# Cross-attention with residual and layer norm: the first chunk loaded in two transfers, the last eight pairs in a new order, the last store in two halves

## The chip, the cores and the metric

The kernel runs on one core of one Trainium2 chip. The metric is device time in microseconds (us) of one execution. Before the change it is 512.98 us, the median of three runs (512.11 to 513.15). Beside the runs there is one profiled execution, whose trace is what the pages below show. The engines are called PE (TensorE, matrix products; PEld is its weight load), DVE (VectorE), ACT (ScalarE), POOL (GpSimd) and SP (SyncE, which here only issues transfers).

## The reference

Queries come from `x` (4 × 2048 rows of 512), keys and values from a context of 4 × 77 rows of 512, with 16 heads of 32. All is float32.

```python
qs = (q @ wq).reshape(Bq, Lq, H, HD).transpose(0, 2, 1, 3)
ks_ = (k @ wk).reshape(Bq, Lk, H, HD).transpose(0, 2, 1, 3)
vs = (v @ wv).reshape(Bq, Lk, H, HD).transpose(0, 2, 1, 3)
scores = jnp.einsum('bhqd,bhkd->bhqk', qs, ks_) / jnp.sqrt(jnp.float32(HD))
scores = jnp.where(mask[:, None, :, :], -jnp.inf, scores)
attn_w = jax.nn.softmax(scores, axis=-1)
attn = jnp.einsum('bhqk,bhkd->bhqd', attn_w, vs)
attn = attn.transpose(0, 2, 1, 3).reshape(Bq, Lq, H * HD)
out = attn @ wo + q
mu = jnp.mean(out, axis=-1, keepdims=True)
var = jnp.mean((out - mu) ** 2, axis=-1, keepdims=True)
return (out - mu) / jnp.sqrt(var + EPS) * gamma + beta
```

## The kernel before, in words

**Tiling.** The 8192 rows of `x` are 64 tiles of 128 rows. Two tiles are a pair (32 pairs), four tiles a group (16 groups, one load of x transposed each). Each float32 factor of a big matrix product is split into a high and a low part, so each product is three matmuls (high·high, low·high, high·low) over four chunks of 128 of the inner 512.

**Order.** Nothing is scheduled by a program: the string `ORDER` is a list of words, one operation each, and every engine executes its own operations in the order of the words. The letter names the operation, the number the tile, pair or group. Further strings fix the buffer of each tile (`SLOTS`) and how many no-ops PE executes between the matmuls of a visit (`PADS`, one sign for each visit, in base 36).

**One tile.** A *visit* of 12 matmuls makes a block of queries for a group (`Q`, line 290; its copy out of PSUM is `q`, on DVE). `S` (line 414) makes a tile's scores in 64 small matmuls. `T` (DVE, line 431) adds the mask and takes the maxima of four heads, `e` (ACT, line 446) the exponentials of four heads with their sums, `r` (DVE, line 456) the reciprocals, `n` (POOL, line 461) the normalisation. `t` (DVE, line 482) transposes the probabilities in blocks of 32. `P` (line 493) regroups them by twelve transfers for each pair; the suffix s, a or g says from which queue, SP's, ACT's or POOL's. `V` (line 507) is the value product of a pair, in two PSUM banks; `a` (ACT, line 536) and `b` (DVE, line 540) split its result. `O` (line 579) is the output projection of a tile, a visit of 12 matmuls. `x` loads the rows of x; the residual is added by DVE on the way out (`+`, line 588), in PSUM by DVE (`$`, line 591), or by PE through an identity ahead of the projection (`X`, line 566).

**Layer norm.** Up to tile 47 it goes in pairs: `s` (DVE statistics), `v` (POOL), `k` (ACT scaling, line 617), `f` (POOL, gamma and beta, lines 621 and 622), `w` (store, SP, line 625). From tile 48 on it goes by single tiles: `s` at lines 630 and 632, `u` (POOL, lines 636 and 637), then either `%` (ACT, line 645) and `f`, or `y` (centring, DVE, line 649) and `z` (finish, DVE, line 652). `@` is `u` and the shift at line 641 together.

**The end.** The last pair's tiles are regrouped one by one: `U` (twelve transfers a tile, line 493 as well) and `W` (line 522), the value product of a single tile, with `c` and `d` in place of `a` and `b`. Tile 63 is normalised in two halves (`h`, `m`, lines 467 and 473).

**The start.** Seven matmuls on constants run first (lines 661 to 664), after three no-ops. SP issues the loads in this order: four chunks of "256 columns of x transposed and 512 of wq" (393 KB each, line 677), the context in two halves (315 KB each, line 679), four chunks of wk (262 KB each, line 681), the mask, the rest of the first x. ACT and DVE split chunk 0 (lines 694 to 699), PE makes the first queries chunk by chunk (line 702, twelve matmuls a chunk), then the keys (line 313).

## Time and profile before

| | us |
|---|---|
| median of three runs | 512.98 |
| the profiled execution's own time | 511.94 |
| its span in the trace | 510.10 |
| first matmul on data starts | 4.60 |
| last matmul ends | 503.43 |
| granted TensorE clock, mean | 0.998 |

The page of the profile gives the busy time of every engine over the span, and the chain of work that ended last. The answer of windows gives the same busy times for chosen stretches: length, then PE, PEld, DVE, ACT and POOL with their instruction counts, the granted clock, the mean busy share of the 16 DMA engines, and GB/s. A timeline row is start, duration, engine, line, operation, output and inputs, shapes, and a count when equal neighbours are drawn together; in brackets stands how long the engine had been idle and what released it. A row on SPq or ACTq is the issue of a transfer, not the transfer. Here the ACT operations around the last exponentials may serve as an example of reading:

```profile
477.72 0.34 ACT L446 ACTIVATE pbuf<-pbuf,nm 128x77 f32<-128x77 f32 x1
477.97 0.19 ACT L446 ACTIVATION_READ_ACCUMULATOR pbuf<-pbuf,nm 128x1 f32 x1
478.06 0.58 ACT L536 CAST AH<-pa 128x512 fp32r<-128x512 f32 x1
```

The last exponential of all is the one at 477.72; it ends with the reading of its sum at 478.16, and ACT goes on with a split of a value product.

### The profile page before, as it was taken

The numbers are of one execution on the slowest core, as the hardware profiler recorded it, in microseconds if no ns is written. First come the engines' busy times: TensorE is split into PE (matmuls) and PEld (weight loads), VectorE is DVE, ScalarE is ACT, GpSimd is POOL, SyncE is SP. The second block draws the span as 40 slices with busy tenths as digits, with TensorE's granted clock in tenths as the row PEclk, the third lists the DMA queues.
The fourth block names the chain that finished last, engine by engine and source line by source line (L and its number), as shares of the span: only waits on it lengthen the run. The fifth ranks groups of instructions, "written<-read, shape, count | busy, mean of one in ns | idle before, by whom it ended". The sixth has DMA issues, their size and how long they took to land.

```text
...
## 1 busy us (share of the span) xinstructions
PE 499.4 (98%) x6835; PEld 384.7 (75%) x6835; DVE 470.7 (92%) x2565; ACT 463.2 (91%) x2221; POOL 421.6 (83%) x389
## 2 busy tenths in 40 slices
...
GB/s 304 399 137 216 191 171 173 251 190 239 267 222 219 189 238 209 200 243 207 229 206 245 200 217 238 187 243 161 218 223 210 225 224 168 174 242 259 176 174 214
DMA packets 58995, 110.95 MB, mean 217 GB/s; under 512 B 9398, under 2 KB 11790, under 8 KB 58886
## 3 DMA queue, kind: packets, MB, share of 16 engines
...
## 4 chain that ended last, share of the span: by engine, by line
PE 79%; POOL 6%; DVE 5%; DMA 4%; ACT 2%; issue 1%; SPq 1%; DVEq 0%; POOLq 0%
PE pq L290 32%; PE po L579 25%; PE sc L414 10%; PE pa L507 9%; DMA PT<-B 3%; ACT pbuf L446 2%; DVE B L482 2%; PE pv L341 2%; POOL PT L493 1%; PE pk L313 1%; DMA stage_a<-wk 1%; DVE pbuf L431 1%; POOL o L621 1%; POOL mvt L637 1%; POOL o L622 1%
## 5 line engine op out<-in xcount | busy, mean ns | idle before, releaser
L446 ACT ACTIVATE pbuf<-pbuf,nm 128x77 f32<-128x77 f32 x1024 | 352.5, 351 | 4.2 <-DVE nm L431 4.0
L446 ACT ACTIVATION_READ_ACCUMULATOR pbuf<-pbuf,nm 128x1 f32 x1024 | 196.2, 192 | 0.0
L431 DVE CUSTOM_DVE_ANT_0 pbuf<-sc,mb 128x77 f32<-128x77 f32 x1024 | 171.3, 233 | 8.0 <-PE sc L414 4.3
L461 POOL TENSOR_TENSOR pbuf<-pbuf,ri 128x1232 f32<-128x1232 f32 x63 | 142.8, 2267 | 30.4 <-DVE ri L456 26.2
L579 PE MATMUL po<-woh,AH 128*128 128x512 f32 x256 | 102.2, 399 | 1.8 <-DVE nm L431 1.4
L290 PE MATMUL pq<-xth,wqh 128*128 128x512 f32 (+1 forms) x256 | 101.3, 396 | 0.3
L579 PE MATMUL po<-woh,AL 128*128 128x512 f32 x256 | 100.0, 391 | 0.2
L579 PE MATMUL po<-wol,AH 128*128 128x512 f32 x256 | 99.8, 390 | 0.0
L482 DVE STREAM_TRANSPOSE B<-pbuf 128x1280 f32<-128x1280 f32 x64 | 95.9, 1500 | 2.9 <-POOL pbuf L473 1.4
L290 PE MATMUL pq<-xtl,wqh 128*128 128x512 f32 (+1 forms) x256 | 98.1, 383 | 0.0
L290 PE MATMUL pq<-xth,wql 128*128 128x512 f32 (+1 forms) x256 | 98.1, 383 | 0.0
L431 DVE DVE_READ_ACCUMULATOR2_ANT nm<- 128x1 f32 x1024 | 84.7, 83 | 0.0
L273 POOL TENSOR_TENSOR xtl<-xtf,xth 128x1024 fp32r<-128x1024 f32 x28 | 67.2, 2406 | 5.8 <-ACT xth L269 5.8
L622 POOL TENSOR_TENSOR o<-o,bet 128x512 f32<-128x512 f32 x52 | 67.2, 1293 | 4.1
L414 PEld LDWEIGHTS sc<-kct,q 32*64 32x64 f32 x4096 | 51.3, 130 | 22.8 <-issue 10.8
L621 POOL TENSOR_TENSOR o<-o,gam 128x512 f32<-128x512 f32 x52 | 68.3, 1314 | 0.2 <-issue 0.2
L414 PE MATMUL sc<-kct,q 32*64 32x77 f32 x4096 | 60.7, 238 | 0.0
L507 PE MATMUL pa<-PT,vsb 96*32 96x256 f32 x992 | 59.7, 382 | 0.0
L579 PEld LDWEIGHTS po<-woh,AH 128*128 128x128 f32 x256 | 48.0, 188 | 14.8 <-PE pa L507 1.0
L290 PEld LDWEIGHTS pq<-xth,wqh 128*128 128x128 f32 x256 | 48.0, 188 | 12.4 <-issue 1.2
L579 PEld LDWEIGHTS po<-woh,AL 128*128 128x128 f32 x256 | 48.0, 188 | 11.5 <-DVE AL L540 1.4
L579 PEld LDWEIGHTS po<-wol,AH 128*128 128x128 f32 x256 | 48.1, 188 | 9.9 <-issue 0.5
...
## 6 DMA issues: line engine op xcount, KB each, us to landing
...
```

The source lines that it names most:

```text
L273: nc.gpsimd.tensor_tensor(l[:, c : c + 2], fx.pop((g, c)), xh[g][:, c : c + 2].bitcast(F32), ALU.subtract)
L290: nc.tensor.matmul(pq, w[:, c, m * P : (m + 1) * P], r[g][:, c, rs], start=(n == 0), stop=(n == 11))
L341: nc.tensor.matmul(pv[: rows.stop - rows.start], ctx_s[c][i][:, rows], v[c], start=(n == 0), stop=(n == 11))
L414: mm = nc.tensor.matmul(sc[j][r0 : r0 + SR, g * NK : (g + 1) * NK], qs[q, g, rs.start + r0 : rs.start + r0 + SR], kct[q, g, t // TPB, keys ...
L431: nc.vector.tensor_tensor_reduce(pb[:, h // 2, (h % 2) * NK : (h % 2 + 1) * NK], scs[t][j][:, g * NK : (g + 1) * NK], mb[:, t % TPB, keys_ ...
L446: nc.scalar.activation(pb[:, h // 2, (h % 2) * NK : (h % 2 + 1) * NK], pb[:, h // 2, (h % 2) * NK : (h % 2 + 1) * NK], AF.Exp, bias=nmax[t ...
L461: nc.gpsimd.tensor_tensor(pv, pv, rv.to_broadcast((P, NP, 2, NK)), ALU.mult)
L482: nc.vector.transpose(bt.rearrange("p c q r -> p q c r"), pbuf[t % NPB].rearrange("p q (c r) -> p q c r", c=5),)
L507: nc.tensor.matmul(pas[b, g // 2][HD * j : HD * (j + 1), (g % 2) * BLK : (g % 2 + 1) * BLK], vsb[:, 2 * b // TPB, h % 2, HD * (h // 2) : H ...
L579: nc.tensor.matmul(pos[t], a[:, c, rs], w[:, c, :], start=(first and c == 0 and n == 0), stop=(c == NC_D - 1 and n == 2),)
L621: nc.gpsimd.tensor_tensor(o, o, gam, ALU.mult)
L622: nc.gpsimd.tensor_tensor(o, o, bet, ALU.add)
```

## The change

It has three parts.

- **Start.** Chunk 0 is loaded by two transfers, 512 of its 768 columns by SP and the last 256 by ACT, ahead of ACT's table load. SP's order becomes context half 0, wk 0, wk 1, context half 1, wk 2, wk 3. Eight matmuls on constants follow one no-op, instead of seven after three.
- **Order.** `ORDER` is new from the transposes of tile 1 on to about pair 7, and from tile 52 to the end. Between these (tiles 18 to 50) the words are the same but for two loads and the slots. `PADS` and `SLOTS` are new accordingly: 1723 no-ops in all instead of 1468. In the last part tile 49's residual is added by DVE instead of PE, tile 48's scaling goes from ACT to DVE (`y48`, `z48`), and tile 62's transpose moves from ahead of tile 63's last exponentials to directly ahead of tile 63's transpose. The transfers are shared out anew: of the 24 of tiles 62 and 63, ACT's queue issues eleven (nine before).
- **End.** Tile 62's statistics come from two passes on ACT with accumulated sums (`=`, `stats_act`) instead of DVE's. Tile 63 is finished and stored in two halves of 256 columns (`>` and `<`), the first stored from SP's queue, the second from ACT's.

The diff, with `ORDER` cut to its changed beginning and end, and `SLOTS` left out:

```diff
-WARM = 7
+WARM = 8
...
 ORDER = """
 R1 R0 R3 E l0 l2 C2 C0 C1 C3 g5 M4.4 A0 M0.1 M12.4 A1 M1.3 A3 M8.4 K2 A2 H2 J3 p i3 g4 J1 K0 i2 S0 I2 j2 S1 T0.1
 e0.1 T0.2 H0 T0.0 j3 e0.0 T1.0 T0.3 e0.2 T1.1 Q4 T1.2 e0.3 F0 T1.3 I0 e1.2 r0 n0 S2 q4 e1.0 S3 T2.3 T2.0 Q7 i5 T2.1
-e1.3 F2 T2.2 j5 t0 e1.1 Q6 i4 F1 g7 r1 Y1 e2.0 F3 L1 T3.2 n1 Q5 x1 T3.1 e2.1 Y0 q6 R2 T3.3 e3.3 j4 t1 B0 e2.3 P0.6s
-x3 e3.1 B2 D0 i7 q7 Z0.s T3.0 P0.10s e3.0 q5 P0.2s S4 P0.7s D2 e3.2 Z3.s S6 T4.0 P0.4s e2.2 G1 B1 g6 G2 Z1.s G0
-Z2.s T4.3 e4.3 P0.3s r3 G3 P0.0s Q9 n3 T4.1 P0.1s T4.2 e4.2 P0.9s D1 P0.8s r2 n2 e4.0 t3 P0.5s Q8 P0.11s e4.1 T6.0
-T6.3 i6 t2 Q10 e6.0 r4 P1.0s T6.2 n4 P1.8s T6.1 e6.1 S5 P1.2s q10 x2 q8 Q11 e6.2 j6 P1.11s T5.3 P1.1s T5.2 e5.3
-P1.10s T5.1 P1.9s t4 j7 e6.3 P1.4s S7 P1.6s Q14 T7.0 P1.7s e7.0 q9 P1.3s r6 T7.3 P1.5s n6 e7.3 T7.2 x0 q11 Q13 g8
-e7.2 T5.0 Z13.s T7.1 g9 e7.1 Z6.s M16.4 Z10.s S9 q13 Z11.s e5.0 q14 V0 r7 t6 n7 e5.1 V1 a0.1 T9.1 e5.2 t7 Q15 a1.0
-b0.1 a1.1 P3.4s r5 T9.2 Z12.s n5 e9.2 b1.0 P3.1s b1.1 P3.8s O2 e9.1 T9.3 P3.2s t5 P3.0s a0.0 P3.5s i8 T9.0 P2.2s S8
-e9.0 +2 j8 P3.3s T8.3 O3 P2.6s e9.3 b0.0 P3.6s T8.1 P3.10s T8.2 i9 P2.8s r9 s2 P3.11s S10 e8.2 j9 P3.9s +3 O1 P3.7s
-T8.0 e8.0 P2.9s q15 s3 P2.3s n9 e8.1 P2.7s T10.0 P2.4s O0 T10.1 e8.3 x7 T10.2 v1 P2.1s +1 g11 e10.0 T10.3 P2.11s
...
+e1.3 F2 T2.2 j5 t0 e1.1 Q6 i4 F1 g7 r1 Y1 e2.0 F3 L1 T3.2 n1 Q5 x1 T3.1 e2.1 q6 T3.3 e3.3 j4 t1 B0 e3.2 T3.0 P0.4s
+q7 x2 e2.3 q5 P0.7s S4 D0 P0.5s e3.0 S6 P0.10s T4.3 P0.0s G0 B2 e3.1 R2 T4.0 g6 P0.2s e4.3 r3 P0.8s G3 n3 P0.11s B1
+e2.2 D2 P0.6s T4.1 T4.2 e4.1 G2 r2 Q8 i7 t3 x11 n2 P0.3s e4.2 P0.9s T6.0 P0.1s T6.2 e4.0 j7 x0 Q9 T6.3 Z13.s t2
+e6.0 Z0.s e6.3 G1 S5 r4 P1.0s T6.1 n4 e6.2 P1.7s q8 Q10 T5.3 P1.6s T5.0 P1.10s e6.1 T5.2 P1.3s T5.1 P1.5s i6 S7 t4
+P1.1s e5.3 Z1.s j6 Q11 P1.11s T7.2 e7.2 P1.9s T7.3 Z2.s q9 P1.8s e7.3 Q13 r6 D1 n6 P1.4s T7.0 P1.2s e7.0 T7.1 g9
+q10 x3 e7.1 Z12.s V0 q13 g8 q11 a0.0 Z11.s r7 e5.0 t6 V1 n7 Z10.s Z7.s e5.1 b0.0 S9 N t7 a1.1 Q12 e5.2 b1.1 P3.9s
+a1.0 P3.5s r5 T9.0 n5 P3.11s e9.0 b1.0 Q14 P3.3s T9.2 Z8.s e9.2 T9.1 P3.2s T9.3 P3.4s e9.3 t5 Y0 S8 P3.10s a0.1 O2
+P3.7s q12 i9 T8.1 P3.0s T8.0 e9.1 P2.3s T8.3 P3.8s q14 Z9.s e8.0 O3 T8.2 P3.1s b0.1 P3.6s e8.3 +2 Z5.s r9 P2.0s n9
+e8.2 S10 +3 P2.7s S11 P2.2s T10.0 e8.1 P2.9s s2 O1 j9 s3 T10.3 e10.3 r8 T10.1 v1 g10 Q15 +1 e10.1 Z4.s t9 P2.6s n8
...
-+45 n50 P24.4s s45 e51.2 g30 P24.0s S52 e51.1 +44 P24.5s P24.2g P24.11s V23 T52.0 i29 M56.4 T52.2 P24.10a j29 T52.3
-S53 a23.1 T52.1 e52.3 Q59 r51 t50 e52.1 n51 g31 P24.6s s44 a23.0 x60 Q58 T53.0 e52.2 P24.9s t51 P24.8s P24.1g e52.0
-P24.3s M60.4 P25.11s T53.2 Q57 P25.4s e53.0 q58 P25.5s r52 T53.1 n52 P25.1s e53.2 b23.0 P25.2s T53.3 S54 P25.10s
-e53.1 w43 v22 T54.0 Q56 e53.3 T54.1 x48 q57 P25.8s P25.3g q59 k42 P25.6s r53 T54.2 e54.1 n53 V24 b23.1 T54.3 e54.3
...
-e58.1 @48 T59.3 x50 t57 P27.9s f44 a26.1 P27.5s O50 a26.0 T59.2 e58.2 P28.8s q60 P28.9s b26.1 P28.5s e59.3 P28.6g
-r58 b26.0 x63 S60 n58 $50 P28.3s e59.1 T60.1 O53 w44 T60.0 P28.1s %48 T60.2 x59 e59.2 P28.10g P28.0s t58 P28.2g
-P28.11s X51 f47 e59.0 x56 T60.3 S61 +53 e60.0 T61.3 O51 r59 T61.2 n59 e60.1 T61.1 s50 e61.2 V27 T61.0 t59 P28.4g
-e60.2 P28.7g f48 S62 s53 P29.8s e61.1 P29.2s T62.0 x58 s51 O52 a27.0 w47 a27.1 y51 w48 e60.3 P29.7g b27.0 P29.9s
-u51 b27.1 P29.6s e61.3 y50 V28 P29.10s P29.1g r60 P29.0g z51 P29.11s e61.0 P29.3g T62.3 x54 n60 T62.2 x52 O55 a28.0
-x62 T62.1 a28.1 r61 P29.5a b28.0 n61 b28.1 e62.1 t60 S63 e62.2 O57 t61 P29.4g e62.0 u50 T63.0 P30.2s @53 e62.3 +55
-P30.6s O56 T63.2 P30.0s P30.5g T63.1 e63.0 P30.10s P30.11g r62 P30.3g s55 P30.8s n62 e63.1 P30.1s $52 X63 w51 T63.3
-e63.3 V29 s52 @55 z50 e63.2 t62 @52 X62 P30.9a O54 h63.0 U62.5g U62.2s $56 a29.1 m63.0 a29.0 h63.1 U62.8s s56
-P30.7a b29.0 m63.1 P30.4a b29.1 %52 O58 u56 t63 %55 f52 U62.4a $54 U62.3a U63.4s y56 U63.11s V30 $58 U63.0s z56
-a30.0 U62.9s U63.10g s58 U62.11a U62.7s U63.7g O59 %53 $57 U62.1s U63.6g a30.1 U63.3g s57 U62.6s U62.10a @58 w52
-b30.0 U63.1a U63.2s b30.1 u57 O61 U63.8a y57 f53 U63.5a s54 U62.0a z57 %58 y54 w57 U63.9a O60 $59 f55 +61 s61 s59
-W62 @61 $60 w55 w53 s60 W63 u54 c62 w50 %61 u59 d62 O62 c63 u60 y59 z59 f61 d63 w59 z54 w56 y60 O63 z60 f58 w61 s62
-w49 w54 y62 w60 s63 u62 w58 y63 u63 z62 z63 w62 w63
++45 n50 P24.4s s45 e51.2 g30 P24.0s S52 e51.1 +44 P24.5s M60.4 P24.9s V23 T52.3 i29 w43 T52.2 P24.3s a23.0 T52.0
+j29 S53 e52.0 T52.1 t50 Q58 P24.10a e52.1 g31 P24.2g r51 T53.2 P24.8s P24.1g s44 e52.3 P24.11s n51 Q56 b23.0 q58
+a23.1 e52.2 T53.1 v22 t51 Q57 e53.1 r52 P25.2s T53.3 n52 k44 P24.6s T53.0 P25.11s e53.0 b23.1 S54 q56 x48 f44 q57
+P25.7s e53.2 Q59 T54.1 T54.0 e53.3 T54.3 t52 w44 e54.3 P25.4g S55 P25.0s P25.3g P25.9s r53 O46 T54.2 i30 n53 x62
...
+P27.3g k42 t57 P27.0g O50 e59.0 P27.2g r58 P28.7g P28.11s T59.1 a26.1 n58 P27.7s T59.3 e59.2 x63 b26.0 S60 P28.9s
+b26.1 e59.1 z48 x53 X51 f42 T60.1 w49 O53 P28.8s T60.0 k47 T60.3 e59.3 T60.2 t58 P28.4g e60.0 S61 P28.10g x55
+P28.2g e60.2 r59 P28.3s O51 T61.3 P28.6g n59 P28.1s +53 e60.1 P28.5s T61.0 w48 T61.2 x56 T61.1 e60.3 S62 f47 P28.0s
+t59 V27 e61.1 r60 T62.1 a27.0 T62.0 n60 P29.9s O52 a27.1 s51 e61.3 P29.11s T62.3 x52 b27.0 w42 e61.2 s53 P29.1g x60
+V28 P29.0g P29.8s $50 k46 P29.7g P29.2s T62.2 P29.6g e61.0 b27.1 P29.4g x54 O55 t60 P29.3g P29.10s a28.0 u51 x59
+a28.1 @53 e62.3 r61 +52 n61 b28.1 O54 e62.1 b28.0 y51 +55 P29.5a f46 t61 e62.2 S63 z51 e62.0 X62 T63.2 w51 O57
+T63.1 w47 e63.1 P30.11g T63.3 P30.2s P30.3g r62 P30.5g P30.1s s52 e63.3 n62 P30.6s s50 P30.0s X63 e63.2 T63.0
+P30.10s V29 s55 P30.8s u50 e63.0 y50 @55 $54 O56 a29.0 @52 z50 P30.4a h63.1 w50 $57 m63.1 a29.1 h63.0 b29.0 P30.9a
+s57 m63.0 P30.7a %55 b29.1 O58 u57 t62 %53 f55 %52 t63 U62.10a U62.2s V30 U62.4a U62.1s U62.8a +58 U63.0s f53 a30.0
+s58 U63.4s O59 U62.0a $56 a30.1 U63.11s b30.0 U62.3a U62.9s s54 U62.11a U62.7s U63.7g U63.1a y57 U63.6g U62.6s
+U63.9a s56 U62.5g U63.8a U63.10g b30.1 O61 U63.2s u56 $59 U63.5a w55 z57 U63.3a @58 O60 y56 w46 f52 %58 +61 s61 s59
+W62 @61 y59 W63 $60 c62 u59 y54 f58 c63 d62 O62 %61 z59 s60 w59 w57 d63 u60 w53 y60 O63 w52 u54 =62 z60 w58 f61 y62
+w60 z54 z56 w54 s63 u62 w61 y63 w56 u63 z62 w62 >63.0 <63.0 >63.1 <63.1
...
-    "i86800000000000000000686c10000cfmmlllllllllmmmmmmmmmmmmmmmmmmkkkkkkkkkkkkkkkkkkkkkkkkkkkkkkkkkjkkk00"
+    "immm0ddddddb111111111111dlllllllmmmmmmmmmmmmmmmmmmmmkkkkkkkkkkkkkkkkkkkkkkkkkkkkkkmmmmmmmmlmmm9mmm00"
...
+    def stats_act(t):
+        mv = mvs[t, 1] = tiny.tile([P, 4], F32, tag="mvt", bufs=64 - LATE, name=f"mvt_{t}")
+        nc.scalar.activation(od[t], pos[t], AF.Copy, scale=-1.0 / D, accum_out=mv[:, 3:4])
+        nc.scalar.activation(od[t], pos[t], AF.Square, bias=mv[:, 3:4], accum_out=mv[:, 1:2])
+        by_act.add(t)
+
     def rsqrt_one(t):
         mv = mvs[t, 1]
-        nc.gpsimd.tensor_tensor(mv[:, 2:3], mv[:, 1:2], eps[:, :1], ALU.add)
+        if t in by_act:
+            nc.gpsimd.tensor_scalar(mv[:, 2:3], mv[:, 1:2], 1.0 / D, EPS, ALU.mult, ALU.add)
+        else:
+            nc.gpsimd.tensor_tensor(mv[:, 2:3], mv[:, 1:2], eps[:, :1], ALU.add)
         nc.gpsimd.tensor_tensor(mv[:, 2:3], mv[:, 2:3], mhalf[:, :1], ALU.pow)
 
     def shift_one(t):
@@ -646,11 +655,22 @@
 
     def centre(t):
         o = pos.get(t, od[t])
-        nc.vector.scalar_tensor_tensor(o, o, mvs[t, 1][:, 0:1], gam, ALU.subtract, ALU.mult)
+        m, op = (3, ALU.add) if t in by_act else (0, ALU.subtract)
+        nc.vector.scalar_tensor_tensor(o, o, mvs[t, 1][:, m : m + 1], gam, op, ALU.mult)
 
     def finish(t):
         nc.vector.scalar_tensor_tensor(od[t], pos.pop(t, od[t]), mvs[t, 1][:, 2:3], bet, ALU.mult, ALU.add)
 
+    def finish_half(t, i):
+        cols = slice(i * D // 2, (i + 1) * D // 2)
+        nc.vector.scalar_tensor_tensor(
+            od[t][:, cols], pos[t][:, cols], mvs[t, 1][:, 2:3], bet[:, cols], ALU.mult, ALU.add
+        )
+
+    def store_half(t, i):
+        cols = slice(i * D // 2, (i + 1) * D // 2)
+        (nc.sync, nc.scalar)[i].dma_start(out[t * P : (t + 1) * P, cols], od[t][:, cols])
+
 
     nc.gpsimd.memset(mhalf, -0.5)
     nc.gpsimd.memset(mneg, -1.0)
@@ -658,7 +678,7 @@
     for pb in pbuf:
         nc.gpsimd.memset(pb[:, :, 2 * NK :], 0.0)
     pw = bank("pw")
-    idle(3)
+    idle(1)
     for i in range(WARM):
         ones = [nc.const_aps.tensor(1.0, (P, n), BF16) for n in (P, 512)]
         nc.tensor.matmul(pw, *ones, start=True, stop=True)
@@ -673,12 +693,14 @@
     qd[0] = buf([P, NG, GRP], F32, "q", name="q_0")
     x0h, x0l = xh[0][:, :, :BLK], xl[0][:, :, :BLK]
     f0 = {c: fx[0, c].rearrange("p c r -> p (c r)").rearrange("p (h c r) -> p h c r", h=2, c=2) for c in (0, 2)}
-    for c in range(NC_D):
+    nc.sync.dma_start(first[0][:, : 2 * BLK], xw0[0, :, : 2 * BLK])
+    nc.scalar.dma_start(first[0][:, 2 * BLK :], xw0[0, :, 2 * BLK :])
+    for c in range(1, NC_D):
         nc.sync.dma_start(first[c], xw0[c])
     for c in range(0, NC_D, 2):
         nc.sync.dma_start(ctx_f[:, c : c + 2, : NB * NK], ctxT[:, c : c + 2])
-    for c in range(NC_D):
-        nc.sync.dma_start(stage_a[:, 1, c], wview(wk, c))
+        for i in (c, c + 1):
+            nc.sync.dma_start(stage_a[:, 1, i], wview(wk, i))
     load_mask(0)
     for c in range(0, NC_D, 2):
         nc.sync.dma_start(f0[c][:, 1], xT0[:, c : c + 2])
@@ -746,6 +768,7 @@
         "u": lambda k, part: rsqrt_one(k), "y": lambda k, part: centre(k), "z": lambda k, part: finish(k),
         "w": lambda k, part: store(k), "*": lambda k, part: hold(k), "#": lambda k, part: residual_late(k),
         "&": lambda k, part: split_hi(k, nc.scalar), "~": lambda k, part: split_lo(k),
+        "=": lambda k, part: stats_act(k), ">": finish_half, "<": store_half,
         "$": lambda k, part: residual_psum(k),
         "@": lambda k, part: (rsqrt_one(k), shift_one(k)), "%": lambda k, part: scale_one(k),
     }
```

88 lines of the change are left out of this document (44 added, 44 removed).

## The prediction

> **What bounds the kernel now.** I read the page first: the busy table and the chain of work that ended last.
>
> ```profile
> PE 499.4 (98%) x6835; PEld 384.7 (75%) x6835; DVE 470.7 (92%) x2565; ACT 463.2 (91%) x2221; POOL 421.6 (83%) x389
> ...
> PE 79%; POOL 6%; DVE 5%; DMA 4%; ACT 2%; issue 1%; SPq 1%; DVEq 0%; POOLq 0%
> ```
>
> PE is busy for 98% of the span, so only about 11 us of it are not matmul time, and some busy time is slow matmul time. The table of busy time by stretches says where these lie; I cut it at the first real matmul (4.59), the first key matmul (11.01), the stretches that the order rewrites (to 131, and from 380.67), the end of the last scores' work (484.41) and the last matmul (503.43).
>
> ```profile
> 0.00:4.59 4.59, 3.14 (x7) 0.87 (x7) 0.42 (x2) 1.74 (x3) 3.40 (x13) 1.00 0.62 191
> 4.59:11.01 6.42, 6.41 (x48) 6.42 (x49) 4.74 (x11) 4.16 (x10) 0.00 (x0) 1.00 1.00 358
> 11.01:18.19 7.18, 7.00 (x51) 6.75 (x49) 6.56 (x16) 4.27 (x11) 2.69 (x5) 1.00 1.07 406
> 18.19:131.00 112.81, 112.45 (x1650) 87.66 (x1652) 103.71 (x637) 106.66 (x527) 81.16 (x58) 1.00 0.73 211
> 131.00:380.67 249.67, 249.67 (x3472) 194.07 (x3470) 235.38 (x1311) 244.43 (x1176) 223.37 (x187) 1.00 0.75 217
> 380.67:484.41 103.74, 102.25 (x1461) 75.38 (x1460) 98.05 (x552) 97.49 (x493) 90.91 (x97) 1.00 0.77 211
> 484.41:503.43 19.02, 18.48 (x157) 13.57 (x156) 18.43 (x35) 4.43 (x7) 17.95 (x28) 1.00 0.56 184
> 503.43:510.10 6.67, 0.00 (x0) 0.00 (x0) 3.39 (x6) 0.00 (x0) 2.16 (x5) 0.82 0.56 216
> ```
>
> The columns are the stretch, its length, and the busy time of PE, PEld, DVE, ACT and POOL. From 131 to 380.67 PE never stops, so nothing outside PE can gain there, and its words are kept. ACT is at 244.43 of 249.67 in that stretch (98%): a second engine is nearly full, and in the last pairs ACT (97.49 of 103.74) and DVE (98.05) are too. The chain of waits shows what a matmul run costs when nothing waits:
>
> ```profile
> 79.02 2.96 PE po L579 x12
> ...
> 351.28 0.88 PE sc L414 x54
> 352.16 1.86 PE pa L507 x32
> ...
> 360.58 5.44 PE po L579 x24
> ```
>
> A visit of 12 matmuls to a projection costs 2.72 (half of 5.44), and 2.96 when it stands alone between other work, so 0.24 is lost per run; a tile's scores cost 0.88, a pair's value product 1.86.
>
> **The change part by part.** *The head.* Here is the timeline of its start:
>
> ```profile
> 0.72 1.28 ACT L696 ACT_TABLE_LOAD   x1 [0.72 <-PEq L802]
> ...
> 1.03 3.14 PE L664 MATMUL pw<-const-bfloat16-1.0 128*128 128x512 bf16 x7 [1.03 <-PEq L802]
> ...
> 4.14 0.71 ACT L696 CAST wqh<-first_xtl 128x256 fp32r<-128x256 f32 x2 [2.13 <-DMA first_xtl<-xw]
> ...
> 4.60 1.22 PE L702 MATMUL pq<-xth,wqh 128*128 128x256 f32 x4 [0.42 <-ACT wqh L696]
> ...
> 6.70 0.64 PE L702 MATMUL pq<-xth,wqh 128*128 128x256 f32 x4
> ...
> 7.17 0.64 PE L702 MATMUL pq<-xtl,wqh 128*128 128x256 f32 x4
> ...
> 10.24 0.62 ACT L251 CAST woh<-stage_a 128x512 fp32r<-128x512 f32 x1 [0.99 <-DMA stage_a<-wk]
> ...
> 11.64 0.19 PEld L313 LDWEIGHTS pk<-ctx_h,wol 128*128 128x128 f32 x1 [0.43 <-DVE wol L252]
> ```
>
> Chunk 0 (393 KB) releases ACT and DVE at 4.14 and PE at 4.60. The edit sends its first 512 columns from SP and the last 256 from ACT's queue. ACT's issue goes ahead of its table load, so the two parts start together; the bytes are the same. The warm-up ends at 4.17 (1.03 + 3.14). One more warm-up costs 3.14/7 = 0.45. The three no-ops ahead of it stand between 0.72, where the engines start, and 1.03, 0.10 each; two dropped return 0.2. So PE is free at 4.42 and cannot gain more than 0.18 however early the data land. Bounds: 0.9 earlier if the first twelve matmuls also run fast sooner (they take 6.70 − 4.60 = 2.10, where later fours take 7.17 − 6.70 = 0.47, so 1.41 for twelve), 0.3 later if data land no sooner and the warm-up delays. I take **−0.15**, by the nearest row, that of the warm-up.
>
> [...] No row of the profile before splits one load in two.
>
> *Keys' weights sooner.* The second half of the context (315 KB) now stands behind two of wk's chunks, so wk chunk 0 lands earlier by 315 KB over the 358 GB/s of the stretch from 4.59, 0.9 us. That covers the 0.43 that PEld waits for the key weights, and ACT's 0.99 wait nearly. What is late next is that second context half, needed for the third of four chunks, 2 × 1.8 us (7.18/4 each) after the first key matmul, and put off by two wk chunks (2 × 262 KB, 1.5 us): covered. Bounds 0 and −0.9: **−0.43**.
>
> *The order after the head, pairs 0 to 7.* The same instructions in another order. For the regroup's issues there is this row:
>
> ```profile
> 480.62 0.59 ACTq L493 DMA_DIRECT2D PT<-B  x1
> ```
>
> Counting run starts up to the value product of pair 6, the new order has thirteen and the old fifteen: −2 × 0.24 = **−0.45**. Against it: the value products of pairs 0 and 1 stand a visit and a tile's scores (2.72 + 0.88 = 3.6) earlier on PE, while pair 1's transposes and its twelve regroup issues of 0.59 come earlier by only about two issues. I price that at **+0.4**, bounds 0 and 2.4 (3.6 − 2 × 0.59). The no-ops between matmuls (more of them in the head, up to 22 for a visit) I price at 0: the visits of the steady part carry 20 and cost 2.72 all the same, hidden behind the matmul before them; without that cover each visit would cost some tenths. Head and start together: −0.15 − 0.43 − 0.45 + 0.4 = **−0.63**.
>
> *The last eight pairs.* What should that stretch cost? These groups count its work:
>
> ```profile
> L579 PE MATMUL po<-wol,AH 128*128 128x512 f32 x60 | 23.4, 390 | 0.0
> L290 PE MATMUL pq<-xth,wqh 128*128 128x512 f32 x40 | 16.1, 403 | 0.0
> L507 PE MATMUL pa<-PT,vsb 96*32 96x256 f32 x256 | 15.5, 382 | 0.0
> L414 PE MATMUL sc<-kct,q 32*64 32x77 f32 x896 | 13.4, 237 | 0.0
> ...
> PE po L579 <- DVE nm L431: 1.4, 2, 0.9
> ...
> 477.87 1.12 PE L566 MATMUL po<-xtl,ident 128*128 128x512 f32 x2
> ...
> 478.43 0.80 PE L579 MATMUL po<-woh,AH 128*128 128x512 f32 x1
> ```
>
> Fifteen plus ten visits (four matmuls of each form) at 2.72, fourteen tiles' scores at 0.88, eight value products at 1.86, four residuals by PE at 0.56 (478.43 − 477.87) and some thirteen lone runs at 0.24 make 68.0 + 12.3 + 14.9 + 2.2 + 3.1 = 100.5, against 103.74: about 3.2 us lost, of which the waits list names only 1.4 outright (maxima on DVE late, the bank not free). The new order puts scores and maxima of each tile so that, summed by their rows, the bank is free when PE comes; it takes X49 off PE (−0.56; an addition in PSUM on DVE replaces it) and one scaling off ACT ahead of the last exponentials (two DVE passes replace it). Against that, the last tile's maxima come later in DVE's own order by these passes, about two of 0.7 net. Bounds: 0 (DVE and ACT are 94% full and hold the end where it was) and −3.8 (3.2 + 0.56). I take half, **−1.8**: no single wait is named for the other part.
>
> *After the last value product of a pair* (484.41 to 503.43): the same five visits and two tiles' products, in the same order; 19.02 is 18.48 busy. What may be late is the regroup of tiles 62 and 63, by these rows:
>
> ```profile
> 487.11 4.41 ACTq L493 DMA_DIRECT2D PT<-B  x4
> ...
> 491.63 0.78 ACT L645 ACTIVATE xth<-po,mvt 128x512 f32<-128x512 f32 x1 [4.15 <-DMA PT<-B]
> 491.65 0.59 ACTq L493 DMA_DIRECT2D PT<-B  x1
> ...
> 495.34 1.95 PE L522 MATMUL pa<-PT,vsb 96*32 96x128 f32 x64
> DMA to landing us min/median/max: 2.3/3.5/4.8
> ```
>
> ACT's last issue goes out at 491.65, behind the 4.15 wait; with the median landing of 3.5 it lands at 495.15, just ahead of the product at 495.34. In the new order tile 62's transpose stands right ahead of tile 63's, so 24 transfers wait for a stretch in which 12 of them had gone before; ACT has eleven, seven of them behind the last conversion. From that conversion's end (some 0.75 after the pair's product) to the tile's product (three visits and some starts, 8.6 after it) is 7.86; less 3.5 for landing leaves 4.36 for seven issues, 0.62 each. A free issue takes 0.59. So it just fits, and I price it at **0**; bounds 0 and +4.6 (below, in the rivals).
>
> *After the last matmul.* The chain to the end now:
>
> ```profile
> 503.21 0.76 DVE L649 SCALAR_TENSOR_TENSOR po<-po,mvt,gam 128x512 f32<-128x512 f32 x1
> 503.88 0.69 DVE L630 BATCH_NORM_STATS2 st<-po 128x6 f32<-128x512 f32 x1
> ...
> 505.48 1.40 DVE L652 SCALAR_TENSOR_TENSOR xtl<-po,mvt,bet 128x512 f32<-128x512 f32 x2
> 506.25 0.99 SPq L625 DMA_DIRECT2D out<-xtl  x2
> ```
>
> Tile 62's statistics go from DVE to two passes on ACT, which is idle here (4.43 busy of 19.02); its centring on DVE waits for them, and two finishes stand behind it and ahead of tile 63's statistics, which start 0.45 after the last matmul now. By the same row durations (0.78 for an ACT pass as at 491.63, 0.7 to 0.76 a DVE pass) they would start 0.55 to 1.05 after it: +0.1 to +0.6. The halved finish lets the last store start half a pass earlier and halves each queue's bytes: −0.3. I take **+0.1**, bounds −0.3 and +0.6.
>
> The sum: −0.63 − 1.8 + 0 + 0.1 = **−2.33**. The profiled execution's own time is 511.94 (span 510.10, and 1.84 around it), so it would become 509.6. The median of the three runs is 512.98, 1.04 above the profiled one; the same difference from it gives **510.6**.
>
> **The rivals.**
>
> *The softmax stream sets the end.* ACT and DVE, not PE's order, decide when the last exponentials come, and reordering PE leaves the 3.2 us where they are. For it: ACT at 98% in the steady stretch. Against: ACT falls to 94% in the last pairs and has one operation less. Then only the head counts: −0.63 + 0.1, **512.4**.
>
> *The bunched regroup makes the last product wait.* If the 24 transfers queue on one another, ACT's seven issues take 1.10 each, as the four at 487.11 do (4.41/4), and land in 4.8, the longest of the row: 7 × 1.10 − (7.86 − 4.8) = 4.6 us of wait on PE ahead of tile 62's product. It decides from the point where that wait passes the 2.33 gained elsewhere, which is 0.96 an issue at a landing of 3.5. Time 512.98 − 2.33 + 4.6 = **515.3**. For it: the old order, with half the transfers in that place, already made ACT wait 4.15 on such a queue. Against: there the wait cost PE nothing.
>
> *The change doesn't do what it says.* Chunk 0's two parts land together when one did, as they share engines, and the last store's halves take as long as the whole. Then the head gives +0.3 for the warm-up instead of −0.15 and the end +0.4: 510.6 + 0.45 + 0.3 = **511.4**, with the last pairs' gain intact.
>
> *The slow matmuls end sooner.* Eight warm-ups with less idle time before them make the first twelve matmuls run at 0.47 a four: −0.7 more, **509.9**. [...] The rows at 4.60 to 6.70 agree that the first matmuls are slow.
>
> **How the numbers follow.** Some 0.2% (1.03 us) is what a measurement of this kernel can tell from no change: faster is under 511.95, slower over 514.0. The forecast, with its own spread of 509 to 511.9, has 0.45; the earlier fast clock 0.06; the split that does nothing 0.13, faster too. The softmax stream has 0.15 (no change), the bunched regroup 0.21, of which 0.02 stops short of 514.0. Adding up: faster 0.64, no change 0.17, slower 0.19. The likeliest gives 510.6. The range starts at 508.4 (the start at its bound, 0.75 more, and all of the 3.2 in the last pairs, 1.4 more) and reaches to 514.6, past no change and into the bunched regroup, leaving out some 0.05 below and 0.14 above.
>
> **What would show it.** In the profile after: the first real matmul at about 4.45; no wait of PEld for the key weights near 11; the stretch from pair 24 to the last value product about 1.8 shorter; no wait at line 507 near pairs 0 and 1 above 0.4; the last tiles' product (line 522) some 9 us after the last pair's product, its releaser not a DMA; the last two store halves issued within a microsecond of each other. The prediction is wrong if PE waits on a regroup ahead of line 522 by more than 2.3, if the early value products wait by over 1 us, or if the last matmul is followed by more than 7.3 us.

## The result, and the profile after

The changed kernel takes 515.07 us (median of 21 runs, 512.9 to 517.3), the kernel before 512.37 in the runs beside it (511.3 to 514.3). The ratio is 1.0054, with an interval of 1.0045 to 1.0064: slower by about 2.8 us, where 2.3 less were forecast. Its runs are also spread over 4.4 us, those of before over 2.9. In the table of experiments one run each of e6_x4_early and e7_old_noops was slow (520.56 us at a mean granted clock of 0.988, 521.20 at 0.987); it counts in the median there and not in the ratio.

The profiled execution of the changed kernel took 515.97 (span 514.20), 0.9 above the median. This is its table of busy times by stretches, cut at the same work as the one of before (first real matmul, first key matmul, last key matmul, value product of pair 5, the start of the rewritten last pairs, value product of the last whole pair, last matmul):

```profile
0.00:4.58 4.58, 3.57 (x8) 1.05 (x9) 0.42 (x2) 1.74 (x3) 3.40 (x13) 1.00 0.57 180
4.58:11.15 6.57, 6.57 (x48) 6.57 (x49) 5.82 (x13) 5.28 (x12) 0.00 (x0) 1.00 1.00 363
11.15:17.88 6.73, 6.73 (x50) 6.73 (x49) 5.48 (x14) 3.29 (x8) 2.96 (x5) 1.00 1.07 406
17.88:133.23 115.35, 112.67 (x1650) 88.39 (x1652) 102.53 (x614) 108.19 (x536) 79.73 (x57) 1.00 0.72 206
133.23:383.09 249.86, 249.86 (x3472) 194.26 (x3470) 235.50 (x1334) 243.11 (x1165) 224.95 (x188) 1.00 0.76 218
383.09:488.20 105.11, 102.21 (x1460) 75.34 (x1459) 99.19 (x556) 97.69 (x493) 88.52 (x96) 1.00 0.77 208
488.20:507.04 18.84, 18.43 (x157) 13.57 (x156) 17.81 (x32) 5.34 (x10) 17.82 (x27) 1.00 0.61 191
507.04:514.20 7.16, 0.00 (x1) 0.00 (x0) 3.90 (x8) 0.00 (x0) 2.71 (x5) 0.81 0.52 196
```

The stretch of pairs 0 to 5 is 115.35 long instead of 112.81, with the same 1650 matmuls: 2.5 us more. The steady stretch is equal to 0.2. The last pairs take 105.11 instead of 103.74 (+1.4) and the end 7.16 instead of 6.67 (+0.5). The keys (6.73 instead of 7.18) and the last pair's visits (18.84 instead of 19.02) gained, and the chunks ahead of the keys lost 0.15 (6.57 instead of 6.42). The page's chain of the changed kernel shows that PE no longer carries the time alone:

```profile
PE 67%; DVE 14%; DMA 6%; SPq 5%; ACT 4%; issue 2%; POOL 2%; DVEq 0%; ACTq 0%
```

PE had 79% before; DVE has gone from 5% to 14%, and the issuing queue of SP from 1% to 5%. One place where this happens is seen in the timeline of the changed kernel around the residual of tile 4 (rows of SP, DVE and PE; those of other instructions are left out):

```profile
103.99 1.38 SPq L625 DMA_DIRECT2D out<-o  x1
...
108.39 0.53 SPq L548 DMA_DIRECT2D o<-x  x1
108.96 1.29 SPq L493 DMA_DIRECT2D PT<-B  x2
...
113.40 0.69 DVE L588 TENSOR_TENSOR o<-po,o 128x512 f32<-128x512 f32 x1 [2.03 <-issue]
114.05 0.94 PE L414 MATMUL sc<-kct,q 32*64 32x77 f32 x64 [0.51 <-DMA PT<-B]
...
117.53 0.90 PE L414 MATMUL sc<-kct,q 32*64 32x77 f32 x58 [0.23 <-DVE nm L431]
```

The x rows of tile 4 land in the buffer that tile 3's output leaves; SP stores that output at 103.99 and issues the load at 108.39. DVE comes to the residual at 111.37 and stands for 2.03 (the profile names no releaser here; in e5_pool_regroups below it names this load). The maxima behind it are late, and PE's scores of tile 15 wait for them at 117.53. The scores of tile 14, at 114.05, wait for a transfer by the profile: in the kernel, scores that stand directly ahead of a value product are held until the regroups of that product have landed (`early_waits`), and the last regroup of pair 4 is issued on SP right behind this load, at 108.96. Before, the same load was issued at 107.11 and used at 116.10, nine us later.

### The profile page after: what moved, and what is told of

It is laid out like the page before. It is cut to its first block, busy times and chain, and to the rows that moved or that the text cites. A ratio compares the mean times of both kernels' runs of the same rounds, so it can differ in the third digit from the quotient of the medians.

```text
span 514.2 us, 22062 instructions
## 1 busy us (share of the span) xinstructions
PE 500.0 (97%) x6834; PEld 385.9 (75%) x6834; DVE 470.7 (92%) x2567; ACT 464.7 (90%) x2224; POOL 420.1 (82%) x388
## 4 chain that ended last, share of the span: by engine, by line
PE 67%; DVE 14%; DMA 6%; SPq 5%; ACT 4%; issue 2%; POOL 2%; DVEq 0%; ACTq 0%
PE pq L290 28%; PE po L579 22%; PE sc L414 8%; PE pa L507 8%; DVE pbuf L431 3%; ACT pbuf L446 3%; SPq L493 3%; DVE B L482 3%; PE pv L341 2%; DMA stage_a<-xT 2%; DMA o<-x 2%; DVE st L630 1%; DMA stage_a<-wk 1%; DVE AL L540 1%; DVE po L659 1%
## 5 line engine op out<-in xcount | busy, mean ns | idle before, releaser
L622 POOL TENSOR_TENSOR o<-o,bet 128x512 f32<-128x512 f32 x51 | 66.0, 1294 | 4.0
L621 POOL TENSOR_TENSOR o<-o,gam 128x512 f32<-128x512 f32 x51 | 67.2, 1318 | 0.4 <-ACT o L617 0.3
L414 PE MATMUL sc<-kct,q 32*64 32x77 f32 x4096 | 61.8, 238 | 2.7 <-DMA PT<-B 1.0
L290 PEld LDWEIGHTS pq<-xth,wql 128*128 128x128 f32 x256 | 48.1, 188 | 9.7
```

What stands on the lines that cost most here:

```text
L290: nc.tensor.matmul(pq, w[:, c, m * P : (m + 1) * P], r[g][:, c, rs], start=(n == 0), stop=(n == 11))
L414: mm = nc.tensor.matmul(sc[j][r0 : r0 + SR, g * NK : (g + 1) * NK], qs[q, g, rs.start + r0 : rs.start + r0 + SR], kct[q, g, t // TPB, keys ...
L621: nc.gpsimd.tensor_tensor(o, o, gam, ALU.mult)
L622: nc.gpsimd.tensor_tensor(o, o, bet, ALU.add)
```

## The experiments

All ratios are against the kernel before, from runs on the same chip. "Pair 6" is where that pair's value product starts (145.6 before), "last pairs" how much longer than before the way from pair 23's product (line 507) to tile 62's (line 522) is; both are from one trace each. The rows ran in four groups on different chips (the kernel before had medians of 512.37 to 512.67 beside them), so the ratios are to be compared rather than the medians.

| | median, us | ratio, 95% interval | pair 6 | last pairs |
|---|---|---|---|---|
| the change | 515.07 | 1.0054 (1.0045 to 1.0064) | 147.9 | +1.0 |
| e1_old_tail | 515.42 | 1.0061 (1.0040 to 1.0082) | 148.8 | −0.1 |
| e2_new_tail_only | 512.99 | 1.0009 (0.9994 to 1.0024) | 146.6 | −1.1 |
| e3_old_loads | 515.02 | 1.0047 (1.0026 to 1.0068) | 148.2 | −0.5 |
| e4_new_loads_only | 512.62 | 1.0001 (0.9988 to 1.0014) | 145.8 | +0.1 |
| e5_pool_regroups | 514.40 | 1.0027 (1.0009 to 1.0045) | 147.2 | −1.6 |
| e6_x4_early | 514.90 | 1.0043 (1.0025 to 1.0062) | 145.9 | −1.1 |
| e7_old_noops | 516.10 | 1.0082 (1.0054 to 1.0110) | 146.4 | −0.6 |
| e8_whole_store | 512.31 | 0.9994 (0.9975 to 1.0012) | 145.8 | −0.1 |
| e9_changed_again | 518.19 (one execution) | | 148.0 | +3.5 |
| e10_changed_third | 514.67 (one execution) | | 148.2 | −0.3 |
| e11_x4_early_again | 513.18 (one execution) | | 146.6 | −0.6 |
| e12_before_again | 511.94 (one execution) | | 145.6 | 0.0 |
| e13_three_fixes | 515.28 | 1.0055 (1.0036 to 1.0074) | 148.8 | −2.2 |
| e14_best_tail | 511.43 | 0.9968 (0.9955 to 0.9980) | 145.4 | −1.9 |
| e15_x55_late | 514.22 | 1.0033 (1.0014 to 1.0052) | 148.8 | −2.1 |
| e16_start_fixes | 516.74 | 1.0080 (1.0056 to 1.0104) | 148.3 | 0.0 |
| e17_x4_and_x55 | 513.17 | 1.0016 (0.9996 to 1.0037) | 147.7 | −2.0 |
| e18_x4_x55_pool | 519.67 | 1.0138 (1.0101 to 1.0175) | 151.6 | −1.9 |

**Which part costs it.** Both kernels have the same words from tile 18 to tile 51, except that more loads moved there than the two that I named: the thirteen loads of x transposed `g14` to `g26` each stand one place later, and so does `x43`. The steady stretch is equal to 0.2 us all the same. So the rewritten start or end of one kernel can be joined to the other kernel's rest, with the buffers renamed at the seam.

```diff
 # e1_old_tail: the change up to +44, then the words of before
 ... e51.1 +44 P24.5s
-M60.4 P24.9s V23 T52.3 ... w62 >63.0 <63.0 >63.1 <63.1
+P24.2g P24.11s V23 T52.0 ... z62 z63 w62 w63
 # e2_new_tail_only: before up to +44, then the words of the change; loads of before
```

> The changed kernel with the words from tile 52 on, their buffers and their no-ops taken back to those of before; the loads at the start and the order of pairs 0 to 7 stay changed. Theory 'start' (the trace after is 2.2 to 2.4 us behind at the value products of pairs 6 to 23 and only about 1.5 more are lost later): 514.1 to 514.7. Theory 'tail' (the rewritten last pairs lose it): 512.2 to 512.8.

> The kernel before with the words from tile 52 on taken from the changed kernel, with the halved last store and the statistics on ScalarE; loads and order of the start as before. Theory 'start': 512.8 to 513.5, since the trace shows 1.0 lost in the last pairs and 0.5 behind the last matmul in an execution that was 0.9 above the median. Theory 'tail': 514.7 to 515.3. My prediction's own step would give 511.

```diff
 # e3_old_loads takes these back in the change, e4_new_loads_only puts them into the kernel before
-    nc.sync.dma_start(first[0][:, : 2 * BLK], xw0[0, :, : 2 * BLK])
-    nc.scalar.dma_start(first[0][:, 2 * BLK :], xw0[0, :, 2 * BLK :])
-    for c in range(1, NC_D):
+    for c in range(NC_D):
         nc.sync.dma_start(first[c], xw0[c])
 ... (also the places of the context and of wk among the loads, WARM and the no-ops)
```

> The changed kernel with the loads, the no-ops and the seven matmuls at the start taken back; both rewritten parts of the order stay. If the loads are to blame (the first scores wait 0.86 us at 21.77 for keys that ScalarE copies only behind a cast that waits for x): 514.3 or less. If the rewritten order is to blame: 514.9 to 515.5, since the key weights are 0.4 later again.

> The kernel before with only the changed loads, no-ops and eight matmuls at the start. If the loads are to blame: 512.9 to 513.2, first scores near 21.8 instead of 21.2 with a wait of about 0.9 ahead of them. If they are harmless: 512.0 to 512.5. My prediction's steps (0.15 and 0.43 less) would give 511.8.

The old last pairs do not help (515.42), and the new ones alone cost nothing that can be told (interval 0.9994 to 1.0024). The new loads alone change nothing (1.0001), and taking them back does not help (515.02). So the loss is in the new order of pairs 0 to 7; the traces of the change, e1_old_tail and e3_old_loads have pair 6's product 2.3 to 3.2 later than before.

**Is it SP's queue, or one load?** Two edits of the changed kernel's words:

```diff
 # e5_pool_regroups: six parts of pair 3, suffix s to g
-P3.10s ... P3.7s ... P3.0s ... P3.8s ... P3.1s ... P3.6s
+P3.10g ... P3.7g ... P3.0g ... P3.8g ... P3.1g ... P3.6g
 # e6_x4_early: two of SP's words earlier; tile 4's x in the buffer planned for tile 5's, and the other way round
-... Z4.s t9 ... T11.3 P4.11s ... w3 Z6.s P4.4s ... a2.1 x4 T12.1
+... Z4.s Z6.s t9 ... T11.3 x4 P4.11s ... w3 P4.4s ... a2.1 T12.1
```

> The changed kernel with six of pair 3's regroup transfers (parts 10, 7, 0, 8, 1, 6) issued from POOL's queue instead of SP's. Theory 'SP queue' (SP issues 48 regroups, the 14 transfers of the values and the x loads back to back from 59 to 113, and what waits on it is late): SP is some 3.7 us earlier by 82, the load of x for tile 4 is issued before 106, the residual of tile 4 no longer waits 2.0, scores near 114 and 117 do not wait: 512.7 to 513.6. Theory 'order of PE and DVE' (PE's visits stand in an order that DVE and ACT cannot follow, whatever the queues): 514.8 to 515.4.

> The changed kernel with one value transfer (Z6) and the load of x for tile 4 moved ahead of pair 4's regroups on SP, in a buffer that is free then; the number of SP's transfers is the same. If that one late load is the cause: DVE's residual of tile 4 has no wait (2.0 before), 513.4 to 514.2. If the whole SP queue is too full: the wait moves to another transfer, 514.6 to 515.4.

With six transfers less, SP still issues that load at 107.54 (108.39 in the change) and DVE still waits 2.28 for it: the full queue as such was not the cause of that wait. The time, 514.40, lies between the two expectations, and its interval (1.0009 to 1.0045) just reaches the changed kernel's. With the load moved, this is the timeline (SP, DVE and PE) of e6_x4_early:

```profile
91.77 0.44 SPq L548 DMA_DIRECT2D o<-x  x1
...
110.69 0.69 DVE L588 TENSOR_TENSOR o<-po,o 128x512 f32<-128x512 f32 x1
...
112.84 0.95 PE L414 MATMUL sc<-kct,q 32*64 32x77 f32 x64
```

The load is out at 91.77, the residual follows without a wait (nothing in brackets), the scores come 1.2 earlier than in the change, and pair 6's product is at 145.9, 2.0 earlier. Not all of that is the load: PE was 0.65 ahead before it came to this place (the projection of tile 7 starts at 104.43, in the change at 105.08). From that projection to the next query visit PE takes 12.04 here and 13.28 in the change, so the load is worth 1.2 us of PE in these two traces. The same way takes 12.01 to 12.05 in all six traces with the load moved (here, e11, e13, e16, e17, e18) and 12.62 to 14.49 in all eight with the new order of the start and the load where it was. The timed runs did not show a gain: 514.90, with an interval that overlaps the changed kernel's. So something more was open.

**No-ops and the last store.**

```diff
 # e7_old_noops: the change with before's no-ops for its first 36 visits
-    "immm0ddddddb111111111111dlllllllmmmm...
+    "i86800000000000000000686c10000cfmmll...
 # e8_whole_store: e2_new_tail_only with one finish and one store for tile 63
-... z62 w62 >63.0 <63.0 >63.1 <63.1
+... z62 w62 z63 w63
```

> The changed kernel with the numbers of no-ops that the kernel before had for its first 36 visits (few or none up to pair 3). Prediction's step (no-ops cost nothing): 514.8 to 515.4. If the 200 no-ops more at the start slow PE by 0.01 us each: 513.

> The kernel before with the new last pairs as in e2_new_tail_only, but tile 63 finished and stored whole from SP's queue. Prediction's step (halving saves 0.3): the span goes on 0.3 longer behind the last matmul than in e2_new_tail_only (7.5 against 7.2), 513.3. If halving saves nothing, as the second half is issued 4.00 after the last matmul where a whole finish would allow some 3.9: 7.0 to 7.2, 512.9.

Fewer no-ops made nothing faster (516.10): the step that priced them at nothing stands. Its interval overlaps the changed kernel's; whether its runs are really slower, though its one trace is not, is open. For the store, the timelines of the changed kernel and of e8_whole_store behind their last matmuls (at 507.04 and 503.50):

```profile
510.14 0.87 DVE L666 SCALAR_TENSOR_TENSOR xtl<-po,mvt,bet 128x256 f32<-128x256 f32 x2
510.26 0.33 SPq L625 DMA_DIRECT2D out<-xtl  x1
510.68 0.38 SPq L672 DMA_DIRECT2D out<-xtl  x1
511.04 0.36 ACTq L672 DMA_DIRECT2D out<-xtl  x1
```

```profile
504.33 0.69 DVE L630 BATCH_NORM_STATS2 st<-po 128x6 f32<-128x512 f32 x1
...
505.94 1.40 DVE L662 SCALAR_TENSOR_TENSOR xtl<-po,mvt,bet 128x512 f32<-128x512 f32 x2
506.71 0.99 SPq L625 DMA_DIRECT2D out<-xtl  x2
```

The second half's issue starts 4.00 behind the last matmul (511.04 − 507.04) and ends at 4.36; the whole store's issue ends at 4.20 (506.71 + 0.99 − 503.50). Two half passes take 0.87 (510.14), one whole pass about 0.7 (half of 1.40). The span goes on for 7.16 and 7.20: halving saved nothing.

**The same kernels once more.**

> The changed kernel once more, for a second trace, since its times are spread from 512.9 to 517.3. Theory 'waits that vary': what the execution is above 511 stands as waits of PE between 60 and 120 and near 465 (2.3 and 1.2 us in the first trace), at the same words as before and of other sizes; PE's busy time stays within 0.5 of 500. Theory 'clock': the waits are the same within 0.3 and the busy time or the slow start of PE differs.

> The changed kernel a third time, with the same expectations as e9_changed_again. With 'waits that vary' the three executions differ by over 1 us in at least one of: the value products of pairs 0 and 1, the residual of tile 4, the value product of pair 28.

> The kernel e6_x4_early once more: its trace had no wait at the residual of tile 4 and took about 512, while its runs had a median of 514.9. Theory 'x4': the residual of tile 4 has no wait again, and the execution is under 513.5. Theory 'full queue': another word waits for its transfer by over 1 us, time 514 to 516.

> The kernel before once more, for the spread of its waits: theory 'waits that vary' needs them to be small here, under 0.3 in all between 60 and 131, as in its first trace (0.1), and the value product of pair 6 within 0.7 of 145.6.

There is no edit in these. The kernel before has pair 6's product at 145.61 both times, but the three kernels with the same start words and loads have it from 145.4 to 146.6 (e14, e8, e2), so a difference of 1 us in that column between two traces says little. Most of that spread stands ahead of the first scores, which start at 20.93 to 22.30 in them: from there to pair 6's product these five traces take 124.3 to 124.6. The changed kernel takes 126.2, 126.3 and 127.3 for the same way, and with the load of tile 4 moved (e6, e11 and e17) 124.6, 125.5 and 124.8. The changed kernel has its wait at tile 4's residual each time (2.03, 2.22, 2.21), and e6_x4_early had none again. But the second execution of the change took 518.19, and lost its time in the last pairs; this is its table by stretches:

```profile
464.00:467.00 3.00, 1.10 (x5) 0.56 (x3) 2.96 (x15) 3.00 (x16) 3.00 (x7) 1.00 0.80 171
467.00:469.00 2.00, 1.88 (x24) 1.32 (x28) 2.00 (x4) 0.97 (x6) 1.82 (x5) 0.64 1.03 314
469.00:471.00 2.00, 2.00 (x18) 0.94 (x10) 0.39 (x1) 0.94 (x3) 1.90 (x2) 0.50 1.09 286
471.00:473.00 2.00, 2.00 (x6) 1.56 (x5) 1.95 (x3) 2.00 (x14) 1.92 (x3) 0.50 0.99 241
473.00:475.00 2.00, 2.00 (x7) 1.58 (x6) 0.00 (x0) 2.00 (x13) 1.18 (x1) 0.65 1.00 206
```

PE waits 2.02 ahead of pair 28's value product (its busy time is 1.10 of the first 3.00), and right behind the wait the granted clock (the third number from the end) falls to 0.50 and stays there until about 474.4. Both of my theories were half right: the waits vary, and behind a long one (2.02) the clock fell to 0.50, which cost more than the wait. From pair 28's product to pair 29's it took 16.31, in e10_changed_third, with the same words at full clock, 13.10: 3.2 us for a wait of 2.02.

**What holds up pair 28.** In the changed kernel's timeline, SP and PE:

```profile
452.39 0.46 SPq L625 DMA_DIRECT2D out<-o  x1
452.90 0.59 SPq L493 DMA_DIRECT2D PT<-B  x1
457.89 0.33 SPq L548 DMA_DIRECT2D o<-x  x1
...
462.81 2.13 SPq L493 DMA_DIRECT2D PT<-B  x3
...
466.54 1.93 PE L507 MATMUL pa<-PT,vsb 96*32 96x256 f32 x32 [1.24 <-DVE nm L431]
```

SP issues nothing from 453.5 to 457.9. Next in its order is the load for tile 55, which needs the buffer of tile 49, whose store was only issued at 452.39; four regroups of pair 28 stand behind it, the last issued at 462.81, 3.7 ahead of the product that needs it. The bracket names DVE for the product's wait; that it was these transfers is what the next edit tests. Tile 55's rows are not used before 474. Four kernels move that load and the next:

```diff
 # e15_x55_late: in the change; e14_best_tail: in e8_whole_store
-... P28.10g x55 P28.2g ... P28.3s ... P28.1s ... P28.5s T61.0 w48 T61.2 x56 T61.1 ... P28.0s t59
+... P28.10g P28.2g ... P28.3s ... P28.1s ... P28.5s T61.0 w48 T61.2 T61.1 ... P28.0s x55 x56 t59
 # e16_start_fixes: e6_x4_early, and pair 1's value product behind the scores of tile 9; e13_three_fixes: all three
-... t6 V1 n7 ... b0.0 S9 N
+... t6 n7 ... b0.0 S9 V1 N
```

> The changed kernel with three moves: Z6 and the load of x for tile 4 earlier as in e6_x4_early, pair 1's value product behind the scores of tile 9, and the loads of x for tiles 55 and 56 behind the last SP regroup of pair 28. If the named waits (value product of pair 1, residual of tile 4, value product of pair 28) are all of the loss: 511.0 to 512.6, no wait of PE over 0.7 behind 60. If something else in the new start costs it: 514 to 515.

> The kernel before with the new last pairs, tile 63 stored whole, and the loads of x for tiles 55 and 56 behind the last SP regroup of pair 28. If the load of tile 55, which waits for the store of tile 49 in whose buffer it lands, holds up pair 28's regroups on SP: no wait ahead of pair 28's value product (1.2 to 2.0 us before), 510.8 to 511.8, faster than both kernels. If the value product waits for other transfers: 512.2 to 512.9.

> The changed kernel with only the loads of x for tiles 55 and 56 moved behind the last SP regroup of pair 28. By the wait that it takes away (1.2 to 2.0 us, and now and then a stretch at half clock): 513.2 to 514.2. If the wait moves on to the next value product: 514.7 to 515.3.

> The changed kernel with only the two moves at the start (Z6 and the load for tile 4, and pair 1's value product behind the scores of tile 9). If these waits are the loss of the start: 512.4 to 513.4. If the new start loses elsewhere: 514.5 to 515.

In e14_best_tail the timeline now reads:

```profile
450.32 3.48 SPq L493 DMA_DIRECT2D PT<-B  x4
453.91 0.68 SPq L625 DMA_DIRECT2D out<-o  x1
454.63 0.58 SPq L493 DMA_DIRECT2D PT<-B  x1
455.31 1.50 SPq L548 DMA_DIRECT2D o<-x  x1
...
462.52 1.93 PE L507 MATMUL pa<-PT,vsb 96*32 96x256 f32 x32
```

SP does not stop, the regroup is out at 454.63, eight us ahead, and the product has no wait. That kernel is faster than both: 511.43, interval 0.9955 to 0.9980. The move alone is worth about 1.3 us there by the ratios (0.9968 against 0.9994 for e8_whole_store) and about 1.1 in the changed kernel (1.0033 against 1.0054); the intervals of each pair overlap, so neither size is sharp.

The other move, pair 1's product behind the scores of tile 9, was a mistake of mine. In e13_three_fixes and e16_start_fixes PE has a new wait there (of e13_three_fixes):

```profile
75.55 0.47 PE L290 MATMUL pq<-xth,wqh 128*128 128x512 f32 x1 [1.93 <-DVE nm L431]
```

The query visit at 75.55 (the word `Q14`) had a bank that pair 1's product leaves in the changed kernel; with the banks planned anew for the later product it has one of the scores of tile 9, and waits 1.93 until DVE has taken their maxima. That is more than the move for tile 4 had given. The last two kernels are without it:

```diff
 # e17_x4_and_x55: e6_x4_early and e15_x55_late together; e18_x4_x55_pool: also three parts of pair 1 from POOL
-P1.8s ... P1.4s ... P1.2s
+P1.8g ... P1.4g ... P1.2g
```

> The changed kernel with the load for tile 4 earlier (as in e6_x4_early) and the loads for tiles 55 and 56 later (as in e15_x55_late), and no other move. If the wait of tile 4's residual, 2.0 to 2.2 us in the traces, is most of the loss of the start: e15_x55_late's 514.2 falls to 512.0 to 512.8. If timed runs lose it elsewhere, as e6_x4_early's 514.9 would say: 513.8 to 514.6.

> As e17_x4_and_x55, with three of pair 1's last regroups (parts 8, 4, 2) issued by POOL, in two gaps of 0.9 and 1.9 us that it has near 63 and 67. If what is left of the loss is the wait of the first two value products on those regroups (0.4 to 1.5 us in the traces): 0.4 to 1.2 less than e17_x4_and_x55. If not, or if POOL is too late with them: the same or up to 1 more.

e17_x4_and_x55 is at 513.17, between the two expectations: by the ratios the two loads together are worth some 1.9 us. Its interval (0.9996 to 1.0037) is clear of the changed kernel's, and it is still not faster than the kernel before. That leaves more than the 0.8 us to the kernel before, since the new last pairs alone gain: e14_best_tail, with the start of before, is 2.5 us faster than e17 by the ratios (0.9968 against 1.0016; it also stores tile 63 whole). So the new start still costs some 2 us with the load moved. In e17's trace, where pair 6's product is 2.1 late, 1.7 of that stands at the first scores, which wait for ACT's last keys:

```profile
22.93 1.80 PE L414 MATMUL sc<-kct,q 32*64 32x77 f32 x128 [1.54 <-ACT kct L326]
```

They start at 21.20 in the kernel before, and at 20.88 to 21.77 in the other traces with the new start, so one trace does not say how much of the timed loss this is.

e18_x4_x55_pool took 519.67, far outside both expectations. Its profile shows why: with three regroups from POOL the second product waits 2.59, longer than in any other trace (the first waits 0.60, as much as in some of them), and the clock falls. Two rows of its timeline, then one of its stretches:

```profile
66.12 1.93 PE L507 MATMUL pa<-PT,vsb 96*32 96x256 f32 x30 [0.60 <-DMA vsb<-v]
70.63 3.64 PE L507 MATMUL pa<-PT,vsb 96*32 96x256 f32 x32 [2.59 <-DMA xtf<-xT]
```

```profile
72.00:74.00 2.00, 2.00 (x24) 0.78 (x16) 2.00 (x3) 0.00 (x0) 0.00 (x0) 0.50 0.11 41
```

The second product takes 3.64 instead of 1.93, at clock 0.50. So pair 1's product seems to stand on the landing of its regroups, as the prediction had it: their queue is all that was edited. POOL issues the last two from 64.64 on, and its three took 4.3 us in the median from issue to landing. The bracket names another transfer, so this is inferred from the edit.

## Why the prediction was wrong

**The step that failed: "The order after the head, pairs 0 to 7".** It was priced at −0.45 for run starts and +0.4 for regroups that the early value products wait on, with 0 and 2.4 as bounds. (Two run starts less are 0.48; the sum took 0.45, which changes nothing.) The waits of these products were near the price: 0.19, 0.20 and 0.68 us in the three traces of the changed kernel, at most 0.94 in the others with its start, e18_x4_x55_pool aside. What I left out was the load of tile 4: the new words bring DVE to its residual 4.7 us earlier (111.37, 116.10 before) and its load 1.3 later (108.39, 107.11). I had gone by the words of PE and DVE and by the regroups, and had not looked at which buffer each load of x lands in, when that buffer's store goes out, and what stands behind the load on SP. DVE stood 2.0 to 2.2 us for it in the three traces of the changed kernel, and PE lost 1.2 to 1.6 by it, of the 1.7 to 2.8 that these traces lose from the first scores to pair 6's product; the six traces with the load moved show no such loss.

How much of it the timed runs carry is not settled. The ratios fall by 0.0011 (e6_x4_early against the change) and by 0.0017 (e17_x4_and_x55 against e15_x55_late), which is 0.6 and 0.9 us, with overlapping intervals. Some 2 us of the new start stay unexplained in the timed runs; the first scores' start and the first products' waits are candidates that no run here separates. The second load, that of tile 55, belongs to the step on the last pairs; there the omission was the same.

The three signs of being wrong that I had named did not come about in the traces of the changed kernel: no wait on a regroup ahead of line 522, no wait of an early product over 1 us, and 7.15 to 7.20 us after the last matmul. It was slower all the same. The signs watched the terms that I had priced, and the loss came in one that I had not.

**Start, −0.15.** ACT's first cast starts at 4.12 instead of 4.14 and the first real matmul at 4.58 instead of 4.60. The rival that the two transfers land together when one did was right here; that they share engines fits the profile of before, where SP's queue alone takes 97.0% of the time of the 16 DMA engines from 2 to 11 us. That of slow first matmuls ending sooner was not: the first twelve took 2.26 (4.58 to 6.84) instead of 2.10, and the table has a granted clock of 1.00 there, before and after; what makes them slow no run shows.

**Keys, −0.43.** The size was right (6.73 for 7.18 in the stretch), but in this trace it was given back at once, by a wait that I had not looked for:

```profile
20.34 1.05 ACT L269 CAST xth<-stage_a 128x1024 fp32r<-128x1024 f32 x1 [2.13 <-DMA stage_a<-xT]
...
21.77 1.47 PE L414 MATMUL sc<-kct,q 32*64 32x77 f32 x99 [0.86 <-ACT kct L326]
```

ACT copies the last keys only behind a cast that waits for x of the second group, and that load did not land earlier. The first scores start at 21.77, where they started at 21.20 before; in the two other traces of the changed kernel they start at 21.64 and 20.88, so the wait comes and goes.

**The last eight pairs, −1.8.** The size was about right: the new order is worth 1.9 to 2.2 us up to tile 62's product where the load of tile 55 is out of the way (e13_three_fixes, e14_best_tail, e15_x55_late, e17_x4_and_x55). Of that, 1.2 to 1.6 lie in the stretch that was priced, up to the last pair's product, and 0.6 to 0.7 behind it, where I had expected 0. Which of the moves brought it no run separates. The rival of the softmax stream, by which reordering gains nothing here, does not hold. As written the order held a wait of its own ahead of pair 28's product, 0.4 to 2.0 us, through SP's queue, which I did not follow there; the first trace ends up at +1.0.

**The regroup of tiles 62 and 63, 0.** No wait came, as priced: tile 62's product comes 8.67 behind the first of the three visits (498.73 − 490.06) with no wait on a transfer, and ACT's queue kept up. The rival of the bunched regroup did not come about; what made the kernel slower lies elsewhere.

**After the last matmul, +0.1.** It was +0.5. The statistics of tile 63 start 0.84 behind the last matmul (0.45 before), inside what I had given, and make up most of it; the 0.3 taken off for the halved store was not there.

**The no-ops, 0.** No run speaks against it: e7_old_noops, with fewer, took 516.10, the change 515.07. The tenths that each visit would cost without cover were an estimate of mine that no run shows.
